# Layer 0's product on four column groups, the maximum read in PSUM, and the expert tail as tasks of the list

## The chip, the core and the metric

The kernel runs on one core of one Trainium2 chip. Its time is the device time of that core in microseconds (us), from repeated executions of the same program. One further execution was recorded by the hardware profiler. All data are 32-bit floats; such a matmul shows as two instructions (two passes) in the trace.

## The reference

Two layers, each cross attention and then a feed-forward part, with a residual addition around each, for 4 batches of 256 rows of 512. The context has 1601 rows of 512 for each batch.

```python
x = x + L0_xattn(layernorm(x), ctx, Wq_d, W_qk, Wkv_d, Wv_u)   # 16 heads, latent keys of 32
x = x + L0_ffn(layernorm(x), weight_q, scale, zero_point, bias)   # int4 weight, dequantised
x = x + L1_xattn(layernorm(x), ctx, Wq, Wk, Wv, Wo)   # 16 heads of 96, 4 key-value heads
x = x + L1_ffn(layernorm(x), W, b, A, Bmat, LiMEs)

# L0_xattn: latents shared by all heads
scores = ((Q @ Wq_d @ W_qk) per head) . (K @ Wkv_d) / sqrt(32)
out = softmax(scores) @ (K @ Wkv_d @ Wv_u) per head
# L1_xattn: hidden = concat([context, latents]); softmax(q k^T / sqrt(96)) v, then @ Wo.T
# L1_ffn: expert weights
H, z = x @ W.T + b, x @ A
H_slice, delta_slice = H[:, 1::2, :8], z[:, 1::2] @ LiMEs.T
logits = 0.5 * H_slice / max|H_slice| + 0.5 * delta_slice / max|delta_slice|   # maxima over all batches
probs = softmax(logits); thresh = second largest
weights = probs * sigmoid((probs - thresh) / 0.5), normalised over the 8 experts
p_mix = repeat(weights, 2) @ LiMEs
return H + (z * p_mix) @ Bmat * 0.5
```

The maxima of H_slice and delta_slice are over all batches, so the last step of layer 1 needs the gate of all four.

## The kernel before

The scores of a head lie with the keys on the partitions and the 256 queries in the free dimension, in 13 key tiles of 128 (layer 0) or 15 (layer 1), in four groups: 4, 4, 3, 2 tiles or 4, 4, 4, 3. `Head.schedule` describes a head:

1. Scores on PE, four row groups of 32 at a time, into PSUM tiles `s` (two buffers of two banks).
2. ACT copies each group into a tile `S` in SBUF (a ring of 8 buffers, four for each head, so two heads).
3. DVE takes the maximum over the tiles (`maxima`, then `last_maximum`); PE turns it (`turn`), DVE reduces it over the keys (`over_keys`), PE spreads it again over the partitions (`spread`), DVE copies it from PSUM to `mB` (`keep`).
4. DVE subtracts `mB` from each group (`subtract`), ACT takes the exponential in place (`weights`).
5. PE multiplies with the values (`product_units`), accumulating over the key tiles. ACT copies the result out (`finish`).

The PSUM tile `o` (two buffers of one bank) holds a head's turned maximum, its spread maximum and, later, its product.

In layer 0 the values are the 32 columns of the latents, and a further 32 columns of ones beside them give the sum of the exponentials. With 64 columns, two key tiles at a time share PE as two column groups: seven units of two matmuls for 13 tiles (`Head0.product_units`). `l0_output` multiplies the product with `wv_h`, whose rows are arranged for the partitions of the two groups, and divides by the sum. In layer 1 the values have 96 columns and one of ones, and take all of PE, one tile at a time.

Nearly all work is a list of tasks. `Plan.order` puts them in an order by hand-given costs, dependences, the reuse of buffers and priorities (`prio`, offsets `AT_...` around the place of a head); nine forward passes with priorities from backward passes between them, and the shortest plan is taken. A forward pass always starts the task that can start first; ties go by priority, and a task of PE whose tiling (`form`) differs from that of the one before has `HOLD` added to its priority. Each engine then runs its tasks in that fixed order. SP issues most DMAs.

The heads follow one written line: layer 0 of batch 0 (16 heads), then three times a mixture of layer 1 of batch b and layer 0 of batch b + 1, then layer 1 of batch 3:

```python
STAGE = "11111001001010010100100101001011"
LINE = " ".join(["0" * H0, STAGE, STAGE, STAGE, "1" * H1])
```

Keys and values of the next context, queries, and the linear products are further tasks, between the heads. The context tile, the keys and the values have one buffer each (the keys one for each group of thirds, the values one for each pair of key-value heads), so those of the next batch can be made when the last heads that read them are through.

At the end of layer 1, `l1_gate` makes the low-rank product z, the gate columns of H and those of delta. z of the first three batches is kept in DRAM (`z_held`), and the rows of the result in `held`. After the list comes code outside it: the maxima, the softmax, the second largest, the sigmoid and the normalised weights of all batches on DVE and ACT; a turn on PE; `mix`, four matmuls that bring the weights to 32 ranks by 4 x 128 pairs of rows; the scaling of `z_all` (32 partitions by 1024); and for each of eight blocks of 128 rows one matmul of 33 rows (32 ranks, one of ones for the bias b1) by 512, an addition to the rows by DVE and a store.

Of the kernel before, what the change touches and what calls it, by code (L numbers as in the profile page):

```python
# [8 lines left out]
F32 = mybir.dt.float32  # L9
# [5 lines left out]
P = 128  # L15
# [46 lines left out]
class Plan:  # L62
# [6 lines left out]
    HOLD = 1.0  # L69
# [4 lines left out]
    def task(self, eng, us, what, deps=(), prio=0.0, new=(), uses=(), lag=0.0, form="full"):  # L74


        t = Task(eng, us, what, [d for d in deps if d is not None], prio, new, len(self.tasks))
        t.lag, t.form = lag, form
        for b in (*new, *uses):
            b.users.append(t)  # L80
        self.tasks.append(t)
        return t
# [122 lines left out]
def xattn_ffn_x2_kernel(  # L205
# [39 lines left out]

    def o_psum(name):
        return psum.tile([P, 2, T], F32, tag="o", bufs=2, name=name)

    def aux_psum(name):
        return psum.tile([P, 512], F32, tag="aux", bufs=2, name=name)  # L250

# [53 lines left out]
    wv_h = const.tile([P, H0, 33], F32, name="wv_h")  # L305
    nc.gpsimd.memset(wv_h, 0.0)
    for r in (0, 64):
        nc.scalar.dma_start(
            out=wv_h[r : r + L0, :, 0:32], in_=wv_u.rearrange("l (h d) -> l h d", d=32)
        )  # L310
        nc.gpsimd.memset(wv_h[r + 32 : r + 33, :, 32:33], 1.0)
# [20 lines left out]
    b1_row = const.tile([R + 1, E], F32, name="b1_row")  # L332
    nc.sync.dma_start(out=b1_row[R : R + 1, :], in_=b1[:, :E])
    limesT_sb = const.tile([R, E], F32, name="limesT_sb")
    nc.sync.dma_start(out=limesT_sb, in_=limesT)
# [3 lines left out]
    for b in range(B):  # L339
        nc.sync.dma_start(out=limes_bd[b * E : (b + 1) * E, b, :], in_=limes)  # L340


    z_held = tc.dram_tile([R, B * T], F32, name="z_held")
    zT = const.tile([R + 1, T], F32, name="zT")
    nc.gpsimd.memset(zT[R : R + 1, :], 1.0)
# [3 lines left out]


    FULL = S // P
    DUP = (FULL + 1) * P - S
# [273 lines left out]
    def l0_latents(b, deps, prio):  # L626
# [38 lines left out]

        def ones():
            ckv.tile = work.tile([P, NK0, 2, L0], F32, tag="ckv", bufs=1, name=f"ckv_{b}")
            nc.gpsimd.memset(ckv.tile[:, :, 1, :], 1.0)

# [8 lines left out]
        def mask():  # L678
            nc.gpsimd.memset(ckv.tile[0:DUP, FULL, :, :], 0.0)

# [90 lines left out]
    def l0_output(b, pair, prio):  # L771
# [4 lines left out]
        def step(ps, q):  # L776
            for j in range(2):
# [3 lines left out]
                    rhs=wv_h[:, 2 * pair + j, :],  # L781
# [32 lines left out]
    def l0_bias(b, norms, prio):  # L814
        bias = Buf("rb", 1)

        def load():
            t = work.tile([P, 3, T], F32, tag="rb", bufs=1, name=f"b0_{b}")
            bias.tile = t.rearrange("p i t -> p (i t)")[:, :D]
            nc.sync.dma_start(out=bias.tile, in_=b0.to_broadcast([P, D]))  # L820
# [293 lines left out]
    def l1_gate(b, xnT, deps, w, prio):  # L1114

        def z_step(ps, c):
            nc.tensor.matmul(
                ps[:R, :T],
# [6 lines left out]
        def z_keep(ps):  # L1125
            nc.scalar.copy(zT[:R, :], ps[:R, :T])
            if b == B - 1:
                nc.scalar.copy(st8[b]["z"].tile[:R, b * T :], ps[:R, :T])

        more = [st8[b]["z"]] if b == B - 1 else []  # L1130
# [3 lines left out]
            [("ACT", 0.7, z_keep, more, book["gates"])],  # L1134
            [*deps, *book["gates"]],
# [4 lines left out]
        book["gates"] = []  # L1140
        if b < B - 1:

            def hold_z():
                nc.sync.dma_start(out=z_held[:, b * T : (b + 1) * T], in_=zT[:R, :])

            t = task("SP", 0.1, hold_z, z, prio, lag=2.5)
            book["gates"].append(t)
            book["held"].append(t)


        def g_step(ps, c):
            if c < NC:
                nc.tensor.matmul(
                    ps[:, :E],
                    lhsT=xnT.tile[:, c, 1:T:2],
                    rhs=w.tile[:, c, :E],
                    start=(c == 0),
                    stop=False,
                )
            else:  # L1160
                nc.tensor.matmul(
                    ps[:, :E],
                    lhsT=zT[R : R + 1, 0:P],
                    rhs=b1_row[R : R + 1, :],
                    start=False,
                    stop=True,
                )

        def g_keep(ps):
            nc.vector.tensor_copy(gate[:, 0, b, :], ps[:, :E])  # L1170

        item(
            f"g_ps_{b}",
            chain(NC + 1, 0.24, g_step),
# [6 lines left out]
        def d_step(ps, c):  # L1181
            nc.tensor.matmul(
                ps[:, :E], lhsT=zT[:R, 1:T:2], rhs=limesT_sb, start=True, stop=True
            )

        def d_keep(ps):
            nc.vector.tensor_copy(gate[:, 1, b, :], ps[:, :E])

        book["gates"] += item(
# [4 lines left out]
            prio,  # L1194
        )
# [12 lines left out]

    AT_KEYS = -4.0
    AT_VALUES = -3.0
    AT_HALF = 1.5
    AT_QUERY = -3.2
    AT_LATENT = -2.8
    AT_START0 = -5.4
    AT_W0 = 0.6
    AT_OUT = -2.0
    AT_EVICT = -0.2
    AT_SCORES = -3.0  # L1220
    AT_COPY = -0.9
    AT_MAX = -1.8
    AT_TURN = -0.9
    AT_SPREAD = -0.5
    AT_SUB0 = -0.8
    AT_SUB1 = -1.0
    AT_EXP0 = -0.2
    AT_EXP1 = -0.4
    AT_PROD = 0.2
    AT_FIN = -2.8  # L1230

    class Head:
# [6 lines left out]
        def schedule(self):  # L1239
# [3 lines left out]
            mx, om, mb = Buf("mx", 2), Buf("o", 2), Buf("mB", 1)  # L1243
# [73 lines left out]
            def turn():  # L1317
                om.tile = o_psum(f"o{self.name}")
# [21 lines left out]
            def keep():  # L1340
# [556 lines left out]
```

## Time and profile before

| | |
|---|---|
| median of 3 runs | 1981.87 us (1981.84 to 1982.26) |
| the profiled execution | 1979.79 us, of which the span from first to last instruction is 1978.0 |
| mean granted clock of PE | 0.982 |
| busy in the span: PE, DVE, ACT, POOL | 1905.7, 1379.7, 1158.3, 119.4 us |
| weight loads (PEld) busy | 1336.7 us |

PE is TensorE's matmuls, PEld its weight loads, which run beside them, DVE is VectorE, ACT ScalarE, POOL GpSimd, SP SyncE. A row of a group reads: line, engine, operation, output<-inputs, shape, count | busy us in all, mean ns of one | idle us of the engine just before these, and what ended that. A table by stretch gives the busy us of each engine between two times, with the number of instructions, the granted clock, the share of the DMA engines and GB/s. Busy time is a union: overlapping instructions of an engine count once.

### The profile page before, as it was taken

How to read it: one execution, taken by the hardware profiler on the slowest of the kernel's cores; microseconds unless marked ns; L12 is line 12 of the kernel's file. 1: busy time of each engine (PE TensorE's matmuls, PEld its weight loads, DVE VectorE, ACT ScalarE, POOL GpSimd, SP SyncE). 2: the span in 40 equal slices, each digit the busy share in tenths (PEclk: the TensorE clock that was granted, in tenths of full speed). 3: DMA queues.
4: the chain of work that ended last, by engine and by line, in shares of the span. 5: the costliest groups of instructions: out<-in, count | busy, mean ns of one | idle time of the engine just before them, and what ended most of it. 6: DMA issues, size and time to landing. Idle time of an engine off the chain costs nothing. (4 is left out here: it accounts for less than half of the span.)

```text
span 1978.0 us, 35851 instructions
## 1 busy us (share of the span) xinstructions
PE 1905.7 (96%) x14745; PEld 1336.7 (68%) x14745; DVE 1379.7 (70%) x2086; ACT 1158.3 (59%) x1752; POOL 119.4 (6%) x171
## 2 busy tenths in 40 slices
PE   6999899999999998999999999999999999999976
PEld 4566677666767776666666786666676678777743
DVE  3987458888887355888887636588879655577743
ACT  3887356776776434667776533567677654455530
POOL 1001200000001000000000100000000010000000
PEclk9999999999999999999999999999999999999986
DMA  7000432211000315220101024212100012221121
GB/s 196 16 12 28 149 86 57 62 38 36 23 9 23 86 54 151 54 62 28 38 15 30 22 65 142 79 50 57 41 25 17 23 46 57 68 70 45 45 60 42
DMA packets 132871, 109.11 MB, mean 55 GB/s; under 512 B 69059, under 2 KB 110179, under 8 KB 132324
## 3 DMA queue, kind: packets, MB, share of 16 engines
q1 hardware_dynamic: 125332, 96.01, 17.6%
q10 hardware_dynamic: 7376, 10.82, 1.7%
q8 instruction: 116, 1.90, 0.4%
q14 instruction: 47, 0.39, 0.1%
HBM read 93.50 MB, written 13.27 MB: 54 GB/s over the span
## 5 line engine op out<-in xcount | busy, mean ns | idle before, releaser
L1272 ACT COPY S<-s 128x1024 f32<-128x1024 f32 (+2 forms) x512 | 447.5, 905 | 300.4 <-PE s L1483 150.0
L1360 ACT ACTIVATE S<-S 128x1024 f32<-128x1024 f32 (+2 forms) x512 | 472.7, 950 | 156.2 <-DVE S L1351 128.8
L1351 DVE TENSOR_TENSOR S<-S,mB 128x1024 f32<-128x1024 f32 (+2 forms) x512 | 544.9, 1109 | 4.4
L1293 DVE TENSOR_TENSOR mx<-mx,S 128x512 f32<-128x512 f32 (+1 forms) x704 | 464.2, 659 | 113.4 <-ACT S L1272 87.2
L1508 PE MATMUL o<-S,v 128*97 128x256 f32 x1920 | 458.6, 382 | 0.6 <-ACT S L1360 0.6
L1508 PEld LDWEIGHTS o<-S,v 128*97 128x97 f32 x1920 | 302.2, 164 | 107.4 <-issue 22.9
L1483 PE MATMUL s<-q,kT_k_ps_c 32*128 32x256 f32 x4320 | 276.3, 383 | 0.0
L1483 PEld LDWEIGHTS s<-q,kT_k_ps_c 32*128 32x128 f32 x4320 | 224.6, 185 | 44.8 <-issue 19.5
L1433 PE MATMUL o<-S,ckv 128*64 128x256 f32 x1664 | 225.2, 389 | 1.5 <-ACT S L1360 1.3
L1433 PEld LDWEIGHTS o<-S,ckv 128*64 128x64 f32 x1664 | 117.0, 137 | 92.5 <-issue 31.2
L1290 DVE TENSOR_TENSOR mx<-S 128x512 f32<-128x512 f32 x128 | 88.7, 693 | 123.7 <-ACT S L1272 123.4
L837 PE MATMUL v_ps<-wvT_sb,ctxT 128*128 128x192 f32 x832 | 160.4, 336 | 0.0
L895 PE MATMUL k_ps_c<-ctxT,wk_sb 128*128 128x384 f32 (+1 forms) x480 | 159.2, 453 | 0.3 <-ACT kTlast_k_ps_c L905 0.3
L837 PEld LDWEIGHTS v_ps<-wvT_sb,ctxT 128*128 128x128 f32 x832 | 136.8, 192 | 22.5 <-issue 15.5
L1406 PE MATMUL s<-q,ckvT 32*128 32x256 f32 x1664 | 148.6, 409 | 0.0
L1406 PEld LDWEIGHTS s<-q,ckvT 32*128 32x128 f32 x1664 | 90.6, 185 | 54.7 <-issue 34.7
L1325 DVE TENSOR_REDUCE m<-o 128x2 f32<-128x256 f32 x128 | 53.5, 418 | 85.5 <-PE o L1321 84.8
L895 PEld LDWEIGHTS k_ps_c<-ctxT,wk_sb 128*128 128x128 f32 x480 | 79.1, 190 | 40.8 <-issue 13.7
L1096 PE MATMUL wo_ps<-wo,oT 128*128 128x512 f32 x192 | 93.6, 609 | 13.1 <-POOL oT L1083 13.1
L905 ACT COPY kT_k_ps_c<-k_ps_c 32x384 f32<-32x384 f32 (+1 forms) x180 | 76.7, 426 | 47.3 <-PE k_ps_c L895 44.8
L986 PE MATMUL q_ps<-xnT_xn_tp_a,wq 128*128 128x256 f32 x384 | 97.6, 386 | 1.9 <-ACT p_q_ps L995 1.9
L1483 PE MATMUL s<-q,kTlast_k_ps_c 32*128 32x256 f32 x1440 | 96.3, 391 | 0.0
(139 smaller groups left out, 1339.1 us busy)
## 6 DMA issues: line engine op xcount, KB each, us to landing
q<-q_rows SPq DMA_DIRECT2D x192, 96.0 KB
wq<-in_wqT SPq DMA_DIRECT2D x48, 192.0 KB
wo<-in_woT SPq DMA_DIRECT2D x16, 576.0 KB
q<-q_rows SPq DMA_DIRECT2D x128, 64.0 KB
ctxT<-in_ctxT ACTq DMA_DIRECT2D x6, 1024.0 KB
q_rows<-p_q_ps SPq DMA_DIRECT2D x48, 128.0 KB
q<-q_rows SPq DMA_DIRECT2D x192, 32.0 KB
rb<-rsums SPq DMA_DIRECT2D x16, 288.0 KB
```

Source lines behind the costliest of these rows:

```text
L837: nc.tensor.matmul(ps[:, : 2 * HD], lhsT=src.tile[:, c, a : a + P], rhs=wvT_sb[:, c, half * 2 * HD : (half + 1) * 2 * HD], start=(c == 0), ...
L895: nc.tensor.matmul(out, lhsT=wk_sb[:, c, i, :], rhs=rhs, start=(c == 0), stop=(c == NC - 1),)
L986: nc.tensor.matmul(ps[:, :T], lhsT=wq.tile[:, c, :], rhs=xnT.tile[:, c, :], start=(c == 0), stop=(c == NC - 1),)
L1096: nc.tensor.matmul(ps, lhsT=oT.tile[:, i, q * P : (q + 1) * P], rhs=wo.tile[:, i, :], start=(i == 0), stop=(i == G - 2),)
L1272: nc.scalar.copy(S4[g].tile[:, :n, :], self.scored(ps[g].tile, g))
L1293: nc.vector.tensor_tensor(mx.tile[:, :w, :], mx.tile[:, :w, :], t[:, a : a + w, :], ALU.max)
L1351: nc.vector.tensor_tensor(s[:, :n, :], s[:, :n, :], mb.tile[:, None, :].to_broadcast([P, n, T]), ALU.subtract,)
L1360: nc.scalar.activation(s[:, :n, :], s[:, :n, :], AF.Exp, scale=self.scale)
L1406: nc.tensor.matmul(pss[2 * step + r // 2][:, 2 * (r % 2) + s % 2, :], lhsT=st8[self.b]["ckvT"].tile[part, s, :], rhs=qr[part, self.h % 2, ...
L1433: nc.tensor.matmul(po[64 * par : 64 * par + 64, :], lhsT=s["ckv"].tile[:, t, :, :].rearrange("p o l -> p (o l)"), rhs=self.S[g].tile[:, i, :],
L1483: nc.tensor.matmul(pss[2 * step + r // 2][:, 2 * (r % 2) + slot % 2, :], lhsT=s["kT", self.kv].tile[part, c, slot, :], rhs=s["q1", self.kv ...
L1508: nc.tensor.matmul(po[:VW, :], lhsT=s["v", j // 2].tile[:, t, j % 2, :], rhs=self.S[g].tile[:, i, :], start=(k == 0), stop=(k == NK1 - 1),)
```

## The change

The change has two halves.

**Heads.** The PSUM tile `o` is parted: `m` (one buffer) for the turned and the spread maximum, `o` (one buffer) for the product. `keep` and `mB` go; `subtract` reads the spread maximum in PSUM. In layer 0 of batches 1 to 3 (`packed`) the product takes five units of four matmuls on four column groups of 32: three groups for the latents of three key tiles, the fourth for the columns of ones. For the fourth, DVE first adds exponentials of several tiles (`add_up`), into slots of `S` that the third and fourth group leave free; five totals stand for 13 tiles. The first two units need the sums of the first two groups, the last unit a third sum. Batch 0 keeps the product on two column groups. There are two tables `wv_h`, one for each arrangement.

```diff
-            t = task("DVE", 0.43, keep, [t], at + AT_SPREAD, [mb], [om])
...
-                    mb.tile[:, None, :].to_broadcast([P, n, T]),
+                    om.tile[:, 1:2, :].to_broadcast([P, n, T]),
                     ALU.subtract,
...
+        PARTS = [
+            (3, slice(2, 4), [(0, slice(0, 2)), (0, slice(2, 4))]),
+            (3, slice(2, 4), [(1, slice(0, 2)), (1, slice(2, 4))]),
+            (2, slice(3, 4), [(2, slice(0, 1)), (2, slice(2, 3)), (3, slice(0, 1))]),
+        ]
+        TERMS = [(3, 2, 0, 1), (3, 3, 0, 1), (2, 1, FULL, None), (3, 1, 0, None), (2, 3, 0, 2)]
...
+                def run(to=to, where=where, parts=parts, first=first):
+                    own = S4[to].tile[:, where, :]
+                    terms = [S4[g].tile[:, at, :] for g, at in parts]
+                    if first:
+                        nc.vector.tensor_tensor(own, terms[0], terms[1], ALU.add)
+                        terms = terms[2:]
+                    for term in terms:
+                        nc.vector.tensor_tensor(own, own, term, ALU.add)
...
+        def units_of_three(self):
...
+            def unit(k, po):
+                steps = [
+                    (s["ckv"].tile[:, t, 0, :], self.S[g].tile[:, i, :], k == 0, 3 * k + r + 3 >= NK0)
+                    for r, (t, g, i) in enumerate(run[3 * k : 3 * k + 3])
+                ]
+                g, i, t, _ = self.TERMS[k]
+                total = (s["ckv"].tile[:, t, 1, :], self.S[g].tile[:, i, :], k == 0, k == 4)
+                for r, (lhsT, rhs, start, stop) in [*enumerate(steps), (3, total)]:
+                    nc.tensor.matmul(
+                        po[32 * r : 32 * r + 32, :], lhsT=lhsT, rhs=rhs, start=start, stop=stop
+                    )
```

**Tail.** z of batch b stays in SBUF on partitions 32 b to 32 b + 31 of `zT`; `z_held` goes. b1 is added to the rows by POOL ahead of layer 1's linear product (`add_bias`, which is `l0_bias` made general), and to the gate columns by DVE as they leave PSUM; the bias matmul of the gate goes. All work from the gate to the stores is now tasks of the list (`experts`). The mix is one matmul to 4 x 32 partitions, its scaling works on 128 partitions by 256. The output takes two rounds of four matmuls of 32 rows, one for each batch on its own row group, and then eight additions and stores. `b_lo` is loaded four times, into four groups of 32 partitions.

```diff
-            nc.vector.tensor_copy(gate[:, 0, b, :], ps[:, :E])
+            nc.vector.tensor_tensor(gate[:, 0, b, :], ps[:, :E], b1_gate, ALU.add)
...
+        def mix(ps, _):
+            nc.tensor.matmul(
+                ps[:, :P],
+                lhsT=limes_bd.rearrange("e b r -> e (b r)"),
+                rhs=wts.tile[: B * E, P : 2 * P],
...
+                for b in range(B):
+                    rows = slice(b * R, (b + 1) * R)
+                    nc.tensor.matmul(
+                        banks[b],
+                        lhsT=zT[rows, q * P : (q + 1) * P],
+                        rhs=b_rows.tile[rows, :],
...
+                a = task("DVE", 0.69, add, [p, *written[b][q]], prio, uses=[*ps, rows[b][q]])
+                task("SP", 0.4, leave, [a], prio, uses=[rows[b][q]], lag=2.5)
```

The offsets of the list get other values, so the order of all tasks changes: `HOLD` goes from 1.0 to 2.1, `AT_QUERY` from -3.2 to -6.7, `AT_LATENT` from -2.8 to -14.4, `AT_OUT` from -2.0 to 8.0, `AT_EXP0` and `AT_EXP1` from -0.2 and -0.4 to -12.1 and -21.7, and others likewise; `AT_SUM` = 4.6 is new. The line of heads stays. At the start, limesT is loaded four times instead of once, and wv_u five times instead of twice.

## The prediction

> **What bounds the kernel now.** I read the page first (busy shares, slices, groups), then the table by stretch, the groups with shapes kept apart, the waits, and the chain that ended last for the tail. The table by stretch, cut where the list of heads changes its mix (us, busy us and instructions of each engine, granted clock, DMA):
>
> ```profile
> 0.00:40.00 40.00, 23.36 (x172) 16.89 (x172) 9.72 (x27) 7.00 (x12) 4.82 (x20) 1.00 0.84 224
> 322.00:600.00 278.00, 276.11 (x2244) 186.40 (x2242) 236.72 (x348) 195.80 (x277) 15.59 (x22) 1.00 0.16 41
> 600.00:798.00 198.00, 192.02 (x1434) 143.44 (x1433) 102.89 (x164) 93.07 (x161) 12.36 (x15) 0.98 0.25 74
> 798.00:1078.00 280.00, 277.83 (x2250) 188.19 (x2248) 238.41 (x348) 196.25 (x278) 15.18 (x22) 0.99 0.15 39
> 1276.00:1556.00 280.00, 278.11 (x2252) 188.26 (x2250) 238.82 (x349) 196.31 (x278) 15.23 (x21) 0.99 0.15 40
> 1907.00:1978.00 71.00, 41.99 (x87) 18.64 (x85) 20.18 (x49) 2.22 (x7) 3.08 (x4) 0.66 0.15 48
> ```
>
> Columns two to five are PE, PEld, DVE, ACT. In the three stretches of 280 us, which I call dense (two layers' heads mixed, 24 heads of which 15 are layer 0's), PE is busy 99% and DVE already 85%. After each, some 198 us hold mostly layer 1 with keys, values and the linear products, and DVE is at 52%. So PE bounds everything from 40 to 1907 us, but in the dense stretches only by a seventh.
>
> The rows that the change touches, with shapes apart:
>
> ```profile
> L1433 PE MATMUL o<-S,ckv 128*64 128x256 f32 x1664 | 225.2, 389 | 1.5 <-ACT S L1360 1.3
> L637 PE MATMUL ckv_ps<-ctxT,wkv_d_sb 128*32 128x128 f32 x416 | 15.4, 282 | 0.1
> L1293 DVE TENSOR_TENSOR mx<-mx,S 128x512 f32<-128x512 f32 x576 | 403.8, 701 | 109.0 <-ACT S L1272 87.2 <-ACT S L1360 1.0 <-DVE mx L1293 0.5
> L1293 DVE TENSOR_TENSOR mx<-mx,S 128x256 f32<-128x256 f32 x128 | 60.4, 472 | 4.4
> L1342 DVE COPY mB<-o 128x256 f32<-128x256 f32 x128 | 53.8, 420 | 41.9 <-PE o L1334 41.4
> L1351 DVE TENSOR_TENSOR S<-S,mB 128x512 f32<-128x512 f32 x64 | 43.8, 684 | 0.0
> L602 DVE TENSOR_TENSOR x<-x,wo_ps 128x512 f32<-128x512 f32 x32 | 21.6, 680 | 21.3 <-PE wo_ps L1096 21.3
> ```
>
> The end of the chain that ended last (start, us, what):
>
> ```profile
> 1957.17 1.92 PE mix L1826 x8
> ...
> 1959.12 1.22 DVE z_all L1835
> 1960.34 0.04 issue
> 1960.39 14.03 PE out_ps L1845 x16
> 1974.42 0.02 issue
> 1974.44 0.69 DVE x L1852
> ```
>
> Gate, mix and output run in a row, with nothing beside them.
>
> **Layer 0's product, 48 heads (three of four batches).** Seven units of two column groups become five of four. A unit now costs 225.2 / (64 x 7) = 0.50 us, so 3.52 a head. L637 is the row with four groups of 32 columns: 15.4 us for 64 units of 128 columns, 0.24 each, so a unit of 256 takes about 0.48, no more than with two groups. Saved: two units, 0.95 to 1.0 a head; I take 1.0 (bounds 0.86, two bare units at their spacing of 0.43, and 1.1). That is 15 us in a dense stretch and 48 in all, if PE stays the bound.
>
> **The sums that pay for it, on DVE.** Per such head three additions of 512 (0.70 each) and two of 256 (0.47): 3.05 us. The copy L1342 goes from every head: 0.42. A dense stretch: 15 x 3.05 - 24 x 0.42 = +35.7, so DVE goes from 238 (mean of three) to 274 us, while PE goes from 277.4 to 262.4. The order turns: DVE has more to do there than PE. It cannot be busy all the time. The best 47 us of before have 43.6 (0.93) with PE as the bound; dependent instructions stand about 0.02 to 0.03 us apart on a mean of 0.68, which leaves at most 0.97. I take 0.955, between the two: 274 / 0.955 = 286.9 us against 279.3, which is 7.6 longer.
>
> PE then has 24 us to spare there, and the list starts whatever is ready, so PE work from the next stretch moves forward. From 600 to 680 us the timeline shows 7.8 us of values of the next context and 3.9 of its second group of keys, whose buffers are free by then: 11.7. The third group of keys (12.1) waits for the last scores of the batch and stays. With one layer 0 head behind the dense stretch (1.0): 7.6 - 11.7 - 1.0 = -5.1 a batch, -15 for three.
>
> **The new waits.** The first two product units now wait for the exponentials of the first two groups and 2.1 us of sums, not for one exponential. Queued behind them on PE are the next scores and fillers in the planned order; behind them on ACT are the copies of scores into the S ring (8 buffers, two heads), since S is freed some 3 us later. The maxima on DVE wait for those copies: these are already DVE's longest waits (L1293 above 87 us, L1290, the first maximum of a head, 123). One buffer for the maximum means that the next head's turn waits for the last subtraction; before, the single mB held the next copy in the same place, so at most the turn, reduction and spread (0.3 + 0.4 + 0.3) come out of hiding, and only where no sums or maxima stand ready. One buffer for the product means that the next head's product waits for one to four ACT copies of 0.37; 2 us or more of scores lie between. I cost both at nothing beyond the 0.955.
>
> **The maximum read in PSUM.** L602 reads one operand from PSUM and takes 680 ns for 512; L1351 reads both from SBUF and takes 684. So no charge. [...]
>
> **Small parts.** The bias matmul of the gate goes: 0.43 us on PE in three batches, -1.3. The added b1 is two POOL additions (L827, 1.65 us each) beside the linear product of 7 us; uncovered they would cost 3.3 a batch. At the start SP issues three more limesT loads at 0.33 us ahead of the planned ones, and the first scores wait for loads on that queue: +1 (0 to 2). ACT issues three more loads of wv at 1.55 us, 4.7 in all, before its first copy at 16.96; its queue is free from 9.4, so 2.9 us of slack are left. The retuned offsets and HOLD change only the order; PE idles 6 us in each 198 us stretch, so I bound them at -6 to +6 a batch and take 0.
>
> **The tail.** From 1960.39 to 1975.13 eight products and additions alternate, 1.7 us each. In two rounds on four row groups the first four products take two passes of 0.85 (clock 0.55 there) and a start, about 1.9, then eight additions at 0.71 follow, 5.7: 7.6 instead of 14.7. The mix is one matmul instead of four (-1.4), its scaling 256 wide instead of 1024 (1.2 to 0.43, -0.8), one scalar operation goes (-0.2). That alone is -9.5. As tasks, gate operations need not wait for the linear product, which ends at 1949.5 while their input stood at 1935.5: latent product 3.5 (cold clock), gate 1.9, the small product and copies 0.8, so they can start at 1941.7, run 5.7, then 2.6 for transpose, mix and scaling with a wait on PE, 1.9 and 5.7 again: last addition at 1957.6, -17.5. I take -16. SP issues eight stores at about 0.4, under the additions' 0.71; it has four loads of b_lo (0.32 each) instead of two loads, now behind the last copy of scores; if they came ahead of the loads of the last rsums at 1915 the tail would lose 1.3. Three stores and a load of z leave SP.
>
> **Sum.** The profiled execution took 1979.8 (span 1978.0), 2.1 under the median. -15.3 - 1.3 + 1 - 16 = -31.6: 1948.2 there, 1950 as a median.
>
> **Rivals.** *PE stays the bound* (0.17): the list packs DVE so well, or moves so many fillers, that all 48 us arrive: -48 - 1.3 + 1 - 17.5 = -66, 1916. For it: PE waits almost nowhere in before. Against: 274 us of DVE in 265.
>
> *DVE takes the body's gain back* (0.13): at a share of 0.93 a dense stretch takes 294.6, +2.6 a batch after fillers; only the tail is left: 1973. A subtraction that is slower from PSUM belongs here too: at 0.06 us each, three times the spread of the rows of 512 (680 to 701 ns), 96 of them are 5.8 us of a dense stretch, 6 of its length, 18 in all: 1968. L602 speaks against it; I give it 0.03 of the 0.13. [...]
>
> *The S ring stalls DVE: slower* (0.16). Sums hold S longer, copies of scores come later, the maxima wait for them, and DVE, now the bound, stays as idle as in the pure layer 0 heads (35.6 of 40 us from 126 to 166). It decides below a share of 0.92: then 274 / 0.92 - 279.3 - 12.7 = 5.8 a batch, 17 for three, eats the tail. At 0.90: +12.4 a batch, 1982 + 37 - 16 = 2003. For it: both waits of the maxima on copies. Against: PE can be fed with fillers, and the additions themselves fill DVE's gaps while the next maximum is turned.
>
> *No change* (0.04): about 0.2% is what this kernel's times can tell apart; the two sides cancel near 1982.
>
> **Numbers.** The forecast (1934 to 1964, shares 0.97 to 0.94) has 0.50. Faster by over 0.2%: 0.50 + 0.17 + 0.13 = 0.80; same 0.04; slower 0.16. The range, 1914 to 1979, takes in nearly all of the faster cases and leaves out the slower one and the edge of the first rival.
>
> **What would show it.** Right: product units of layer 0 at 0.5 us, five a head; about 146 us of new DVE additions; dense stretches of 285 to 288 us with DVE at 0.95 and PE near 0.96; the stretches behind them shorter by 12; eight additions in a row at the end, 18 to 29 us before today's. Wrong: units that cost more with four groups; subtractions longer than 1.24 us for 1024; DVE under 0.92 with waits on copies of scores; a gate that still runs behind the linear product; or PE at 0.99 in dense stretches of 265.

## The result and the profile after

The changed kernel takes 1959.18 us (median of 4 runs, 1955.84 to 1960.36) against 1981.86 beside it: ratio 0.9883, 95% interval 0.9866 to 0.99. It is faster, by 22.7 us where 32 were forecast. Its profiled execution took 1958.11 us with a span of 1956.3, 21.7 less than before.

The table by stretch of the changed kernel, cut at the same places in the list of heads as before (us, busy us of PE, PEld, DVE, ACT, POOL, granted clock, DMA):

```profile
0.00:40.00 40.00, 18.74 (x160) 14.36 (x161) 8.32 (x25) 5.47 (x11) 5.17 (x21) 0.98 0.85 218
321.00:611.00 290.00, 281.93 (x2449) 190.35 (x2451) 260.63 (x391) 199.54 (x291) 12.43 (x21) 0.98 0.16 42
611.00:799.00 188.00, 182.12 (x1403) 136.25 (x1402) 110.90 (x172) 90.75 (x151) 13.66 (x18) 0.99 0.29 82
799.00:1076.00 277.00, 274.16 (x2436) 185.73 (x2435) 255.31 (x388) 196.97 (x287) 11.27 (x21) 1.00 0.14 38
1266.00:1544.00 278.00, 274.14 (x2439) 185.61 (x2437) 256.95 (x387) 197.34 (x288) 11.91 (x21) 1.00 0.15 38
1897.00:1956.30 59.30, 29.70 (x81) 13.67 (x79) 18.69 (x48) 2.14 (x6) 5.75 (x6) 0.74 0.19 60
```

In the second and fourth row DVE is busy 261 and 255 us instead of 237 and 238, and PE still 0.97 to 0.99. The rows of the change in the heads, shapes apart:

```profile
L1666 PE MATMUL o<-S,ckv 128*32 128x256 f32 x1728 | 128.9, 384 | 2.1 <-DVE S L1611 2.1
L1640 PE MATMUL o<-S,ckv 128*64 128x256 f32 x416 | 54.2, 386 | 0.0
L1611 DVE TENSOR_TENSOR S<-S,S 128x512 f32<-128x512 f32 x96 | 67.9, 707 | 5.8
L1608 DVE TENSOR_TENSOR S<-S 128x512 f32<-128x512 f32 x48 | 32.8, 684 | 0.0
L1441 DVE TENSOR_TENSOR mx<-mx,S 128x512 f32<-128x512 f32 x576 | 412.6, 716 | 82.2 <-ACT S L1420 60.5
L1441 DVE TENSOR_TENSOR mx<-mx,S 128x256 f32<-128x256 f32 x128 | 54.4, 425 | 4.4
L1494 DVE TENSOR_TENSOR S<-S,pm 128x1024 f32<-128x1024 f32 x320 | 377.9, 1215 | 48.5 <-PE pm L1482 47.8
L1494 DVE TENSOR_TENSOR S<-S,pm 128x512 f32<-128x512 f32 x64 | 43.5, 680 | 0.0
```

L1640 is batch 0's product on two column groups, L1666 the packed one, L1608 and L1611 the sums (those of 512), L1441 the maxima, L1494 the subtraction with the maximum in PSUM. The chain that ended last (start, us, what), from the gate to the last addition:

```profile
1938.62 0.18 DVE inv L1219
...
1943.65 0.46 PE wts_tp L1283
...
1944.47 0.80 PE mix L1292 x2
1945.30 0.43 DVE zT L1303
...
1945.78 2.17 PE out_ps L1333 x8
...
1952.20 0.60 DVE x L1346
```

Cut where groups of heads end (the last matmul of their products), and the rest of the span as the tail, the 21.7 us come from these places:

| us | before | after | difference |
|---|---|---|---|
| heads 0 to 3 | 85.5 | 95.3 | +9.8 |
| heads 4 to 15 | 130.3 | 114.9 | -15.4 |
| heads 16 to 19 | 106.5 | 110.5 | +4.0 |
| three dense stretches | 278.0, 280.3, 280.0 | 290.2, 277.3, 277.9 | +12.2, -3.0, -2.1 |
| behind them | 197.6, 197.8, 350.8 | 187.9, 190.3, 353.1 | -9.7, -7.5, +2.3 |
| tail | 71.2 | 58.9 | -12.3 |

### The profile page after: what moved, and what is told of

It is laid out like the page before. It is cut to its first block, busy times and chain, and to the rows that moved or that the text cites. A ratio compares the mean times of both kernels' runs of the same rounds, so it can differ in the third digit from the quotient of the medians.

```text
span 1956.3 us, 37116 instructions
## 1 busy us (share of the span) xinstructions
PE 1867.8 (95%) x15211; PEld 1314.1 (67%) x15211; DVE 1445.2 (74%) x2197; ACT 1152.2 (59%) x1751; POOL 116.0 (6%) x179
## 4 chain that ended last, share of the span: by engine, by line
PE 76%; DVE 11%; DMA 4%; issue 4%; SPq 2%; ACT 2%; POOL 1%; ACTq 0%; DVEq 0%; POOLq 0%
PE o L1744 20%; PE s L1719 15%; PE v_ps L842 6%; PE k_ps_c L900 6%; PE s L1568 5%; PE o L1666 4%; DVE mx L1441 4%; PE wo_ps L1101 4%; DVE S L1494 3%; PE q_ps L991 3%; PE f L615 2%; PE o L1640 2%; PE pm L1469 2%; PE pm L1482 1%; DVE S L1611 1%
## 5 line engine op out<-in xcount | busy, mean ns | idle before, releaser
L1494 DVE TENSOR_TENSOR S<-S,pm 128x1024 f32<-128x1024 f32 (+2 forms) x512 | 529.5, 1081 | 48.5 <-PE pm L1482 47.8
L1441 DVE TENSOR_TENSOR mx<-mx,S 128x512 f32<-128x512 f32 (+1 forms) x704 | 467.0, 663 | 86.6 <-ACT S L1420 60.5
L1719 PE MATMUL s<-q,kT_k_ps_c 32*128 32x256 f32 x4320 | 287.5, 388 | 3.4 <-ACT S L1420 2.1
L1719 PEld LDWEIGHTS s<-q,kT_k_ps_c 32*128 32x128 f32 x4320 | 232.1, 187 | 53.7 <-issue 20.4
L1438 DVE TENSOR_TENSOR mx<-S 128x512 f32<-128x512 f32 x128 | 92.8, 725 | 79.7 <-ACT S L1420 79.4
L1568 PEld LDWEIGHTS s<-q,ckvT 32*128 32x128 f32 x1664 | 93.4, 186 | 56.3 <-issue 23.9
L1666 PE MATMUL o<-S,ckv 128*32 128x256 f32 x1728 | 128.9, 384 | 2.1 <-DVE S L1611 2.1
L1101 PE MATMUL wo_ps<-wo,oT 128*128 128x512 f32 x192 | 98.1, 629 | 16.2 <-POOL oT L1088 16.2
L1473 DVE TENSOR_REDUCE m<-pm 128x2 f32<-128x256 f32 x128 | 53.8, 420 | 77.0 <-PE pm L1469 76.7
L851 ACT COPY v<-v_ps 128x192 f32<-128x192 f32 x120 | 38.2, 321 | 114.4 <-PE v_ps L842 108.3
L1611 DVE TENSOR_TENSOR S<-S,S 128x512 f32<-128x512 f32 x144 | 88.3, 613 | 11.2 <-ACT S L1420 0.5
```

The source lines that it names most:

```text
L1101: nc.tensor.matmul(ps, lhsT=oT.tile[:, i, q * P : (q + 1) * P], rhs=wo.tile[:, i, :], start=(i == 0), stop=(i == G - 2),)
L1441: nc.vector.tensor_tensor(mx.tile[:, :w, :], mx.tile[:, :w, :], t[:, a : a + w, :], ALU.max)
L1494: nc.vector.tensor_tensor(s[:, :n, :], s[:, :n, :], om.tile[:, 1:2, :].to_broadcast([P, n, T]), ALU.subtract,)
L1568: nc.tensor.matmul(pss[2 * step + r // 2][:, 2 * (r % 2) + s % 2, :], lhsT=st8[self.b]["ckvT"].tile[part, s, :], rhs=qr[part, self.h % 2, ...
L1666: nc.tensor.matmul(po[32 * r : 32 * r + 32, :], lhsT=lhsT, rhs=rhs, start=start, stop=stop)
L1719: nc.tensor.matmul(pss[2 * step + r // 2][:, 2 * (r % 2) + slot % 2, :], lhsT=s["kT", self.kv].tile[part, c, slot, :], rhs=s["q1", self.kv ...
```

## The experiments

Three things had to be told apart. First, what bounds the dense stretches: DVE, whose sums took the product's gain, as the prediction had it, or still PE, which shows 0.99 there. Then, what the +9.8 at the start are, which the prediction had at +1; and why the tail gave 12.3 and not 16. All differences below are medians against 1959.18, unless a profile is named; the kernel before ran at 1980.0 to 1982.8 beside them, so a difference of under 3 us between two rows tells nothing.

| kernel | us | against the changed kernel | ratio to before, 95% interval |
|---|---|---|---|
| late_wv | 1953.83 | -5.4 | 0.986 (0.9838 to 0.9882) |
| late_all | 1951.89 | -7.3 | 0.9848 (0.9826 to 0.9869) |
| z_first | 1955.13 | -4.1 | 0.9864 (0.9845 to 0.9883) |
| late_z | 1948.75 | -10.4 | 0.9831 (0.981 to 0.9851) |
| late_z2 | 1943.92 | -15.3 | 0.9817 (0.9801 to 0.9833) |
| no_sums | 1940.19 | -19.0 | 0.9788 (0.9773 to 0.9803) |
| copy_back | 1998.22 | +39.0 | 1.0077 (1.006 to 1.0094) |
| packed_all | 1979.64 | +20.5 | 0.9994 (0.9983 to 1.0006) |
| pool_sums | 1972.01 | +12.8 | 0.9947 (0.9928 to 0.9966) |
| two_groups | 1981.50 | +22.3 | 0.9996 (0.9987 to 1.0006) |
| old_offsets | 1982.76 | +23.6 | 1.0007 (0.9996 to 1.0018) |
| before_new_offsets | 1988.92 | +29.7 | 1.0044 (1.0031 to 1.0057) |

### What bounds the dense stretches

**no_sums** leaves the sums out.

```diff
                 def run(to=to, where=where, parts=parts, first=first):
+                    return
...
-                g, i, t, _ = self.TERMS[k]
+                g, i, t = [(1, 2, 0), (1, 3, 0), (2, 1, FULL), (3, 1, 0), (3, 0, 0)][k]
```

> Leaves out all five sums of exponentials of every packed head (240 additions, 142.7 us of DVE in the profile of the changed kernel); the packed product's matmuls read single tiles in their place, so the values differ, while the counts of every other instruction and the order of each engine stay as they are. Theory A (PE bounds the dense stretches, where DVE at a share of 0.90 to 0.92 still has room): the dense stretches of 277 to 290 us lose at most 3 us each, PE stays at 0.97 or above, and the whole run becomes 0 to 10 us shorter than the changed kernel, 1949 to 1959. Theory B (DVE bounds the dense stretches, as the prediction had it): DVE loses 15 x 2.9 = 43 us in each of them, PE takes over, and the run becomes 15 to 30 us shorter. Theory C (it is the wait for the sums, not DVE's work, that holds PE): PE's idle time of 88 us falls by over 20.

**copy_back** puts a copy of the maximum to SBUF back.

```diff
+                if g == 0:
+                    nc.vector.tensor_copy(mx.tile[:, 1, :], om.tile[:, 1, :])
                 nc.vector.tensor_tensor(
...
-                    om.tile[:, 1:2, :].to_broadcast([P, n, T]),
+                    mx.tile[:, 1:2, :].to_broadcast([P, n, T]),
```

> Puts back one copy per head of the spread maximum from PSUM to SBUF on DVE (0.42 us each, 128 heads, 54 us in all), and the subtractions read that copy; everything else and the order of each engine as in the changed kernel. Theory A (DVE has room in the dense stretches): +0 to 8 us, of which most in the stretches of pure layer 0 heads, where DVE is at its limit (16 heads, up to 7 us). Theory B (DVE bounds the dense stretches): 24 x 0.42 / 0.92 = 11 us more in each, 33 in three, and with the first heads some 40. Subtractions of 1024 are 1.24 us as before if PSUM costs less, 1.21 if the place of the operand is not what made them shorter.

The table by stretch of no_sums, its second and third dense stretch:

```profile
790.00:1063.00 273.00, 271.82 (x2440) 185.61 (x2443) 216.92 (x314) 196.56 (x287) 11.02 (x21) 1.00 0.14 38
1252.00:1524.00 272.00, 270.89 (x2436) 185.09 (x2434) 217.69 (x313) 196.11 (x286) 11.40 (x21) 1.00 0.15 39
```

And the same two of copy_back:

```profile
816.30:1104.30 288.00, 280.05 (x2440) 187.78 (x2440) 268.69 (x412) 197.83 (x288) 13.67 (x21) 0.99 0.14 36
1297.60:1582.40 284.80, 276.94 (x2440) 185.34 (x2440) 268.42 (x411) 197.57 (x288) 12.74 (x21) 1.00 0.14 37
```

Theory B held with both totals: -19.0, and +39.0 where some 40 stood. Per dense stretch the 43 us of sums taken from DVE shorten it by 10.1, 4.4 and 5.4 us, all of the run's 19. The 10.1 us of copies added lengthen it by 5.8, 10.7 and 6.9, 23.4 us where 33 were forecast; 11.5 more come from the stretches behind them, for which nothing had been forecast, so that the total came out is partly luck. The stretch stands at a knee. Below it lies 272.5 us, PE's floor in this order (280 in the first stretch); above it three quarters of what DVE gets arrive (23.4 of 30.2 us). With the copy DVE is at 0.92 to 0.94, the most seen in this order, against 0.90 to 0.92 in the changed kernel. DVE's instructions set the length of the dense stretches, but PE's floor is only 5 us below (10 in the first).

Theory C, a wait for the sums, holds for a part only. PE's idle time fell by 5 us, from 88 to 83, and not by 20. But idle time did not show all of the waiting here, as the next paragraph says. The two kernels run the same matmuls in the same order, so the distance of each matmul's start from the start before it can be compared. Of the 19.9 us in the three stretches, 8.9 lie ahead of the matmuls that turn and spread a maximum, and 6.3 ahead of the product units that need a new sum (the first and the last of five; 1.0 ahead of the other three). So DVE comes late with the maxima above all, and at most a third is the wait for sums.

PE's busy share had said otherwise. The three kernels run the same 15211 matmuls in the same order, and their busy PE is 1854.1 (no sums), 1867.8 (changed) and 1884.4 us (with the copy). Part of this is the clock (mean granted 0.983, 0.981 and 0.978). In the third dense stretch, where it is 1.00 in all three, the records of the matmuls add up to nearly the same (936, 937 and 937 us; a matmul of the packed product takes 384 ns in each), but the busy PE, their union, is 271, 274 and 277. So the records overlap by 665, 663 and 660 us: with more work on DVE they overlapped less, and PE's busy time grew by 6 us with no more matmuls. PE's share was 0.99 in the changed kernel, where DVE's sums still cost 5 us of the stretch, so that share did not show that PE is the bound; the counter-experiment did.

**packed_all** packs batch 0 too, where all heads are layer 0's.

```diff
-            return b > 0
+            return True
```

> The changed kernel with the packed product in the first batch as well (16 more heads on three column groups and one of sums; the order planned anew with the same offsets). Heads 0 to 15 are all layer 0's, with DVE at 0.92, 0.89 and 0.74 and ACT at 0.87 to 0.90 in heads 4 to 15 (114.9 us). Theory A (DVE sets the time where it comes to 0.92): these twelve heads get 12 x 2.97 = 36 us of sums on a DVE that is 98 us busy in 114.9, so they take 134 / 0.93 = 144 us, 29 more, and the run 20 to 35 us longer, 1979 to 1994. Theory B (PE sets it everywhere and DVE finds room): 16 x 0.88 = 14 us less for PE, 1945 to 1950.

Its heads 4 to 15 in the table by stretch:

```profile
104.30:245.20 140.90, 126.74 (x1059) 81.53 (x1063) 127.09 (x206) 98.49 (x163) 7.36 (x17) 0.95 0.15 49
```

Heads 4 to 15 took 140.9 us (144 expected) instead of 114.9, with DVE's work up from 97.2 to 127.1 and PE with 14 us to wait. With DVE at 0.90 here, the packing cost nearly what its sums cost, 26 us for 30 of DVE's: theory A, +20.5 in all. The profile has other differences too: heads 0 to 3 took 9.0 us more, heads 16 to 19 8.9 less, and the first dense stretch 280.2 instead of 290.2, with the same sums in it.

**pool_sums** moves the third sum, two additions of 256, to POOL.

```diff
+                    eng = nc.gpsimd if where == slice(3, 4) else nc.vector
...
-                        nc.vector.tensor_tensor(own, own, term, ALU.add)
+                        eng.tensor_tensor(own, own, term, ALU.add)
```

> The third of the three partial sums of a packed head (two additions of 256, 0.45 and 0.43 us on DVE, 42 us in all) on POOL, every engine's order otherwise as in the changed kernel. From POOL's additions of 512 (1.58 us) one of 256 should take about 0.8. Theory A (DVE sets the dense stretches and PE's floor stands 5 us below, at 273, as the run without sums showed): the dense stretches lose 3 to 6 us each, PE idles less, and the run becomes 10 to 17 us shorter than the changed kernel, 1942 to 1949. Theory B (the dense stretches hang on the wait for the sums, which here come 0.7 us later, not on DVE's work): 0 to 10 us longer. Theory C (POOL's additions lengthen DVE's beside them): DVE's maxima and subtractions show means over 0.67 and 1.08 us, and nothing is gained.

Groups of instructions of this kernel, shapes apart (L1612 is L1611 of the changed one):

```profile
L1441 DVE TENSOR_TENSOR mx<-mx,S 128x512 f32<-128x512 f32 x576 | 434.8, 755 | 83.8 <-ACT S L1420 61.7 <-ACT S L1503 0.5
L1494 DVE TENSOR_TENSOR S<-S,pm 128x1024 f32<-128x1024 f32 x320 | 378.1, 1216 | 55.4 <-PE pm L1482 54.6
L1612 DVE TENSOR_TENSOR S<-S,S 128x512 f32<-128x512 f32 x96 | 77.4, 807 | 6.6 <-ACT S L1503 0.7 <-ACT sums L1790 0.5
L1441 DVE TENSOR_TENSOR mx<-mx,S 128x256 f32<-128x256 f32 x128 | 59.2, 463 | 4.4
L1612 POOL TENSOR_TENSOR S<-S,S 128x256 f32<-128x256 f32 x48 | 47.4, 988 | 12.4 <-ACT S L1503 9.2
```

Theory C, but for the subtraction. POOL takes 0.99 us for what took DVE 0.43, and some of DVE's instructions with both operands in SBUF grow: maxima of 512 from 716 to 755 ns (22 us in all), sums from 707 to 807, maxima of 256 from 425 to 463. A head's first maximum (L1438), with both operands in SBUF too, does not (725 to 724), nor does the subtraction, with one operand in PSUM (1215 to 1216). DVE's busy time is 1450.1 us against 1445.2 although 42 us of work left it. Theory B is not what happened: in the second and third dense stretch, 4.4 and 5.2 us longer, the matmuls that turn a maximum come 5.5 and 4.1 us later in all, those of the products 0.8 sooner and 0.5 later. The profiled execution was the fastest, at 1961.91; the trace accounts for its 3.8 us, not for the other 10 of the median.

### What the parts of the change are worth

**two_groups** keeps the product on two column groups everywhere.

```diff
-            return b > 0
+            return False
```

> Layer 0's product stays on two column groups in all four batches, without the sums of exponentials (the planner orders anew with the same offsets); the maximum read in PSUM, gate, mix and output as in the changed kernel. Theory A (PE bounds the body): PE has 42 us more to do, so the run is 25 to 42 us longer than the changed kernel, 1984 to 2001, that is, the tail's and the maximum's gain are lost to the longer start and nothing else is left against the kernel before. Theory B (the packed product brings the prediction's 5 us a batch, since DVE's sums eat the rest): 12 to 20 us longer, 1971 to 1979.

**old_offsets** is the changed kernel with the offsets of before, **before_new_offsets** the kernel before with the new ones.

```diff
-HOLD = 2.1
+HOLD = 1.0
...
-    AT_EXP1 = -21.7
+    AT_EXP1 = -0.4
```

> The changed kernel with the planner's offsets and HOLD of the kernel before (the sums' offset, which that one lacks, at 0); the same instructions in another order. If the retuned offsets only fit the order to the new costs, as the prediction assumed: within 6 us a batch, that is 1941 to 1977. If they carry the gain (the sums need a place of their own in the order of DVE): 20 us longer or more, above 1979, with the dense stretches longer than 290 us and DVE waiting there for copies of scores.

> The kernel before with the changed kernel's offsets and HOLD and nothing else of the change: the same instructions as before in another order. The changed kernel with the old offsets took 1982.8, 23.6 us more than with its own. Theory A (the new offsets only fit the order to the new costs, above all to a DVE that has 0.90 to 0.92 to do in the dense stretches): here they gain nothing, 1976 to 2000. Theory B (the new order is better by itself, for instance in how fillers are spread, whatever the product does): 1958 to 1970. The first 20 heads tell it by themselves, since the product of the first batch is the same in both kernels: there the changed kernel took 130.3 us less 16.1 for heads 4 to 15 and 4.0 more for heads 16 to 19.

Packing is worth 22.3 us in its final setting, between the two theories: without it nothing is left of the change against before (ratio 0.9996), though the tail is 61.4 us instead of 71.2 in that profile. The same holds for the offsets: without them nothing is left either (1.0007), and on the old instructions they cost 8.9 us (1988.92 against 1979.99). Theory A of that run held. Where in the run this happens, the profiles tell (us):

| | before | before_new_offsets | old_offsets | two_groups | changed |
|---|---|---|---|---|---|
| heads 0 to 19 | 322.3 | 333.9 | 342.1 | 321.9 | 320.7 |
| heads 20 to 127 | 1584.5 | 1581.9 | 1579.6 | 1595.9 | 1576.7 |
| tail | 71.2 | 71.3 | 59.4 | 61.4 | 58.9 |

The offsets are worth 21.4 us in heads 0 to 19, whose product is not packed, and in the 108 heads behind them only 2.9 on the new instructions and 2.6 on the old. So these runs do not show that the packed product needs the new order. On the old instructions that order even has dense stretches of 274.2, 275.3 and 275.1 us, the last two 2 to 3 shorter than the changed kernel's, though with other fillers in them. Packing is worth 19.2 us in heads 20 to 127, but two_groups takes 11.4 more there than before: each of these kernels has an order of its own, and in two_groups PE waits 20.4 us for the scaled output ahead of `wo_ps`, against 13.1 before and 12.3 in before_new_offsets. Against before the heads 20 to 127 gain 7.8. No run has single PSUM buffers as the only difference, so what those cost stays open.

It was not in the dense stretches that the old offsets lost time, as I had expected: those took 282.1, 276.8 and 277.9 us there, the first 8.1 less than with the new ones. Heads 16 to 19 took 129.4 us instead of 110.5, with waits of PE (us in all, times, longest) that the retuned order does not have:

```profile
PE ckv_ps L642 <- DMA ctxT<-in_ctxT: 5.8, 2, 3.5
PE f L615 <- POOL w0T L593: 4.1, 1, 4.1
PE xn_tp_a L510 <- DVE xn_a L500: 3.4, 1, 3.4
```

The granted clock was 0.92 in that stretch, against 1.00. Heads 4 to 15 took 123.3 instead of 114.9, the stretches of 44 to 51 and 76 to 83 another 4 and 8 more.

### The start

**late_wv** loads the pieces of `wv` for three column groups from SP, behind a store that comes after the first heads, **late_all** does so with b1 for the gate and `limesT` too.

```diff
-        for r in rows:
+        for r in rows if name == "wv_2" else ():
             nc.scalar.dma_start(
...
         def keep():
             nc.sync.dma_start(out=w0_held, in_=w.tile.rearrange("p c n -> p (c n)"))
+            for r in (0, 32, 64):
+                nc.sync.dma_start(
+                    out=wv_h[1][r : r + L0, :, 0:32], in_=wv_u.rearrange("l (h d) -> l h d", d=32)
+                )
```

> The changed kernel with the three loads of the second table wv_3 (first used at about 340 us) moved from the ACT queue at the start to SP, behind the store of w0. The order of all tasks stays. Theory A (the 1536 short pieces of these loads hold up the loads on SP: q arrives 4 us late, PE idles 4.5 us and then runs 12 us at half clock): the first four heads end near 87 us instead of 95.3, the kernel is 7 to 10 us faster than the changed one, near 1950. Theory B (the four us come from SP's own extra small loads and from the new order of the first loads): 0 to 2 us.

> As late_wv, and the loads of limesT (four) and of the gate's bias moved to the same later place. Theory A: a further 0 to 2 us, because SP then comes to its first q loads 1.9 us sooner; 8 to 11 us in all against the changed kernel. Theory B1 (the small loads on SP are the cause): nearly all of the 8 to 10 us comes here and not in late_wv. Theory B2 (the order is the cause): neither gains more than 2.

PE's waits in the changed kernel up to 60 us (us in all, times, longest) have one on a DMA:

```profile
PE s L1568 <- DMA q<-q_rows: 4.5, 1, 4.5
```

and SP's queue up to 45 us has a wait that the kernel before does not have (L334 loads `wk_sb`):

```profile
SPq L334 <- DMA wv<-in_wv_u: 5.2, 4, 3.8
```

The changed kernel's row from 40 to 52 us in the table by stretch:

```profile
40.00:52.00 12.00, 12.00 (x45) 7.17 (x46) 6.54 (x8) 3.70 (x6) 2.80 (x3) 0.50 0.35 114
```

The same row of late_all:

```profile
40.00:52.00 12.00, 9.87 (x67) 5.42 (x65) 11.02 (x14) 7.77 (x13) 2.97 (x3) 1.00 0.21 60
```

The loads of `wv` are issued by ACT, but SP's loads wait for them (5.2 us ahead of L334), and the queries, later in SP's order, come 3.5 us later; PE idles 4.5 us, and then runs at a granted clock of 0.50 for 12 us, with 45 matmuls where before did 85. A wait of SP for `wv` (3.0 to 5.8 us) stands in the eight profiles of kernels that have the added loads at the start, and in none of the six that have not. With the loads out of the way the first scores start at 35.5 (late_wv) and 34.4 us (late_all) instead of 39.2, heads 0 to 3 end at 89.8 and 87.3 us instead of 95.3, the clock is 1.00 from 46 us on in late_wv and throughout in late_all, and the gain stays to the end. It is 5.4 and 7.3 us by the median: theory A, though less than the 7 to 10 and 8 to 11 that it gave. Single profiles of these four heads differ by 2 to 3 us. In this order heads 0 to 3 end at 93.4 to 95.3 us in four kernels with the added loads (changed, z_first, no_sums, pool_sums) and at 87.3 to 90.4 in four without (late_wv, late_all, late_z, late_z2), so the loads cost 3 to 8 us there. They are not all that the start hangs on. In late_z2, without them, PE still waits 3.6 us for the queries and runs at a clock of 0.50 to 0.62 from 30 to 46 us; before_new_offsets, without them, ends heads 0 to 3 at 95.7, and old_offsets, with them, at 89.4.

### The tail

**z_first** puts the latent product and the small gate products ahead of the linear product in the last batch (g, z and d are the tasks of the gate's three products, f0 and f1 those of the linear one), and **late_z** is that with late_all.

```diff
+        block = [*g[:-1], *z, g[-1], f0[0], *d, blank, *gate_tasks[:2], *f0[1:-1], f0[-1]]
+        block += [*gate_tasks[2:], *f1]
```

> The changed kernel with one stretch of its list rearranged by hand: of the last batch, the latent product z, its small product and the gate tasks stand ahead of the linear product on PE and of its additions on DVE, all else in the order of the changed kernel. Theory A (the tail is set by the gate chain, which waits behind the linear product): gate chain starts at about 1931 instead of 1937.7, last addition 5 to 7 us earlier, 1952. Theory B (PE is cold there and the linear product, now last, ends as late as the chain did): under 2 us.

> late_all and z_first together. If both causes stand and lie in different places: their sum, 13 to 17 us against the changed kernel, near 1943. If the start's loss is made up later anyway (the middle is bound by other things): only the part of z_first, near 1952.

**late_z2** also puts the gate's comparison ahead of the first linear addition on DVE.

```diff
+        peaks, highest, compare, first_exp, rank, second_exp, weigh = gate_tasks
+        block = [*g[:-1], *z, g[-1], f0[0], *d, blank, peaks, highest, *f0[1:-1], compare, first_exp]
+        block += [f0[-1], rank, second_exp, *f1[:-1], weigh, f1[-1]]
```

> Best version so far: the loads of wv, b1 and limesT late as in the kernel that took 1951.9, the latent product ahead of the linear product as in the one that took 1948.8, and now on DVE the gate's comparison ahead of the first linear addition, which there stood in its way for 2.4 us (the maximum over partitions was there at 1928.5, the comparison began at 1930.9). If the gate's chain then runs beside the linear product, as the prediction's other bound for the tail had it: transpose and mix 1.9 to 2.4 us earlier, the tail behind the last product 54 to 55 us instead of 56.3 and 58.9, and 1945 to 1948 in all. If the maximum over partitions only came at 1930.9 (POOL's span being rough): no gain, 1948 to 1950, and DVE idles from 1928 to 1930.9.

The chain that ended last in late_z2:

```profile
1923.87 3.55 PE z_ps L1132 x8
1927.42 2.01 PE f L624 x2
1929.42 0.33 PE d_ps L1176 x2
1929.75 2.79 PE f L624 x6
...
1936.38 0.60 DVE x L616
...
1937.22 0.50 PE mix L1309 x2
1937.74 0.43 DVE zT L1320
...
1938.21 1.22 PE out_ps L1350 x8
```

z_first moved the gate's input 6.3 us ahead (the delta columns left PSUM at 1931.4 instead of 1937.7; 4.9 counted from the start of the tail), but its tail was 57.2 us, 1.7 less, and the run 4.1 instead of 5 to 7: on DVE the comparison stood behind an addition that waited for PE until 1934.1. late_z, at -10.4, is near the sum of late_all and z_first (-11.4) and short of the 13 to 17 forecast, as each part had given less. With the comparison first the chain runs beside the linear product, and the tail is 53.4 us, 5.5 less than in the changed kernel. PE has no long wait ahead of the output any more (6.0 us for the weights in the changed kernel), and the eight products in the chain take 1.22 us instead of 2.17, at a granted clock of 1.00 instead of 0.50. late_z2 takes 1943.92 us, the fastest kernel here that leaves nothing out: 36 us less than before, 15 less than the change.

## Why the prediction was right, and where its terms were off

The sign and the forecast (1950, with 1934 to 1964 for the case itself) held; its sum of -31.6 came out as -21.7 in the profile. The body from head 20 on gave -7.8 where -15.3 stood, the tail -12.3 where -16 stood. Heads 0 to 19 gave -1.6 where +1 stood, and there luck helped: a start that cost 9.8 and an order and a missing copy that gained 11.4 cancel, and neither was foreseen. By its own steps:

**The product, -1.0 a head.** Measured -0.88: (225.2 - 54.2 - 128.9) / 48. Units of four column groups took 0.54 us, not 0.48 to 0.50; without sums they took 0.52 in the third dense stretch (38.9 us for 75), so part of it is late feeding. Inside the bounds (0.86 to 1.1).

**The sums, 3.05 a head, and the copy, -0.42.** Measured 142.7 us for 48 heads, 2.97 each, and 53.8 of copies gone. But DVE's work in the second dense stretch rose by 17, not 35.7. The durations there add up to 45.2 of sums less 10.1 of copies; five subtractions and three maxima of the same heads fell outside the stretch (7.4), records overlapped by 3.7 more, and the rest, 7, is mostly shorter instructions (23 ns on average for a subtraction, 14 for a maximum of 512, 64 for a head's last maximum). This is the term that was mis-sized.

**A share of 0.955 and 287 us.** Measured 0.90, 0.92, 0.92 and 290, 277, 278. The share was too high (0.92 to 0.94 is the most that the copy forced), the work too large; 255 / 0.92 is 277. So the second and third stretch became 3.0 and 2.1 us shorter, where 7.6 longer was forecast. "DVE has more to do there than PE" did not hold in busy time: DVE was busy 255 to 257 us, and PE, with its fillers and without the sums (no_sums), 271 to 272. What held is that DVE's work sets the length, by 5 us over PE's floor and not by 12. The first stretch has a cost of its own, told at the end.

**Fillers, -12.7 behind each dense stretch.** Measured -9.7, -7.5 and +2.3. They did move forward: in the second dense stretch PE has 24.8 us of values and 25.0 of keys, before 16.9 and 23.5, so 9.4 where 11.7 was forecast. Behind the third, heads 108 to 111 took 6.0 us less, heads 112 to 115 15.0 more and heads 116 to 127 6.8 less; PE waits there for wq (2.8 us at 1624) and for the scaled output (2.4 at 1633). No run tells why the order left those two waits.

**Order, 0.** The step that failed most, though the sum hardly shows it. The offsets were held to be worth 0, within 6 us a batch; they are worth 23.6 with the new instructions and cost 8.9 with the old. From head 20 on the bound held (2.9 and 2.6 us in all); it failed in heads 0 to 19, for which no step stood in the sum. Heads 4 to 19 gained 11.4. Heads 4 to 15 alone took 130.3 us before, 126.2 with the new offsets alone, 123.3 with the new instructions in the old order and 114.9 with both.

**The start, +1.** Measured +9.8, of which the added loads are 3 to 8. ACT's slack of 2.9 us was set against its own issues, but SP's loads waited 5.2 us for the same transfers. That PE would wait 4.5 us, and run at a granted clock of 0.50 for 12 us behind it, stood nowhere in the term.

**The new waits, 0.** PE stood idle for 2.1 us waiting for sums in the whole run (L1666 above), but in the dense stretches the units that need them came up to 6.3 us later than without sums, so the term is not 0. DVE's longest waits, the maxima on copies of scores, fell rather than rose (L1441 82 us idle ahead, before 109; the first maximum of a head 80, before 124).

**The maximum in PSUM, no charge.** It gains a little: 1215 ns against 1239 for 1024, 680 against 684 for 512, and with the operand back in SBUF (copy_back) 1246 and 683. The rows of 1024 before and in copy_back:

```profile
L1351 DVE TENSOR_TENSOR S<-S,mB 128x1024 f32<-128x1024 f32 x320 | 383.0, 1239 | 4.4
L1496 DVE TENSOR_TENSOR S<-S,mx 128x1024 f32<-128x1024 f32 x320 | 388.1, 1246 | 4.4
```

The 0.06 us by which a rival had each subtraction slower from PSUM do not show.

**The tail, -16.** Measured -12.3. From the mix to the last addition it took 8.3 us instead of 18.0, which is the -9.5 of the first bound; eight additions in a row end it, 22 us before the last one of before. The rest was to come from a gate beside the linear product, and the planned order put z behind it; "a gate that still runs behind the linear product" had been named as what would be wrong. late_z2 shows the other bound: 71.2 - 53.4 = 17.8, where 17.5 was worked out.

**The rivals.** With all sums gone the run reaches 1940, not 1916; PE is idle for 83 us of it, most of that outside the dense stretches. The share fell to 0.90 to 0.92, where the slower rival was to decide, and nothing was slower, since its 274 us of work were 255; copy_back and packed_all show how near it was.

## What to carry over

Two engines at 0.9 and above stood at a knee here: price a change there by adding and taking away work on each, since a busy TensorE share of 0.99 (274 of 277 us) was also what late feeding looked like here. When work moves between engines, the planned order is part of the change; here no order was neutral, and it mattered most in heads that the change had hardly touched. Cost it as a range as wide as the gain. A load that is "hidden" has to be hidden on every queue that its transfer delays: SP waited 5.2 us here for loads that ACT had issued. An idle TensorE is to be priced with what came behind it: at the start 4.5 us of idle time were followed by 12 us at a granted clock of 0.50, though not every idle time in this trace was followed by a lower clock.

## What the runs showed of the hardware

In the first dense stretch, in windows of 2 us:

```profile
334.00:336.00 2.00, 0.91 (x11) 0.48 (x10) 1.96 (x3) 1.98 (x4) 0.00 (x0) 1.00 0.61 200
336.00:338.00 2.00, 2.00 (x20) 1.34 (x18) 1.83 (x4) 2.00 (x4) 1.22 (x1) 1.00 0.41 92
338.00:340.00 2.00, 0.81 (x7) 0.52 (x8) 1.90 (x3) 0.45 (x1) 1.08 (x2) 0.66 0.29 88
340.00:342.00 2.00, 2.00 (x24) 1.68 (x17) 1.37 (x2) 0.00 (x0) 0.00 (x0) 0.50 0.67 167
346.00:348.00 2.00, 2.00 (x34) 0.99 (x36) 0.18 (x1) 1.27 (x3) 0.00 (x0) 1.00 0.00 0
```

Two idle times of PE of 1.1 and 1.2 us within 5 us, both with DVE busy, were followed by a granted clock of 0.50 to 0.66 for some 6 us; behind 1.0 and 1.6 us from 452 us on it was 0.50 to 0.67. Of two single idle times of 2.1 us, the one at 690 us was followed by 0.50 (694 to 696 us) and the one at 748 us by 1.00. The first dense stretch is 12.6 us longer than the other two; by these numbers some 5 would be PE's idle time (1.1 + 1.2 + 1.0 + 1.6) and some 6 the clock (twice 6 us at about half), an estimate. The sums are not the only cause: without them the clock was 0.87 at the head of that stretch as well, and with them the stretch took 280.2 us in packed_all. What sets it stays open.
